# Four mixing layers on one core: long scan pieces beside attention, images normalised ahead, softmax reciprocals by DMA, convolutions summed in place

## The chip, the cores and the metric

The kernel runs on one core of a Trainium2 chip. The metric is the device time of one execution in microseconds: the median of three runs was 4425.56 us (4419.15 to 4431.18). The core has a matrix engine (TensorE, PE in the profile, with its weight loads as PEld), three engines for elementwise work (VectorE or DVE, ScalarE or ACT, GpSimd or POOL), and a queue for transfers (SyncE or SP). Each engine works through its own instructions in the order in which they were issued and waits on semaphores of the others.

## The reference

Four layers follow one another on x of shape (4, 128, 64, 64); each adds its result to x, computed on a group-normalised x. All is float32.

```python
def reference(x, ...):
    ...
    x = x + _L0_conv_ref(_gn(x), ...)   # attention
    x = x + _L1_conv_ref(_gn(x), ...)   # 5x5 convolution
    x = x + _L2_conv_ref(_gn(x), ...)   # selective scan
    x = x + _L3_conv_ref(_gn(x), ...)   # 3x3 convolution
    return x

# layer 0, n = 4096 pixels, c = 128
    scores = jnp.einsum('bic,bjc->bij', q, k) * scale
    attn = jax.nn.softmax(scores, axis=-1)
    out = jnp.einsum('bij,bjc->bic', attn, v)

# layer 2, for each half of the channels (one of them with the pixels reversed)
    delta = jax.nn.softplus(xt @ Wd + bd)
    dA = jnp.exp(delta[..., None] * A)
    dBx = (delta * xt)[..., None] * Bm[:, :, None, :]
    _, h = jax.lax.associative_scan(combine, (dA, dBx), axis=1)   # h = dA * h + dBx
    y = jnp.einsum('bldn,bln->bld', h, Cm) + Dp * xt
```

In layer 3 the branch that depends on an offset returns the same convolution either way.

## The kernel before

Channels lie on the 128 partitions, pixels along the free dimension. A matmul produces 128 x 512 (one PSUM bank of eight); CH = 1024 pixels is a chunk, MM = 512 half of one.

The scan is the long part. `scan_core` walks through 4 images x 256 = 1024 ticks. In tick i ScalarE makes the decay `da` (`decay`, L1261, an exponential), GpSimd the drive `db` (`drive`, L1268), VectorE runs the recurrence over 1024 pixels (`recur`, scan L1278), the product with `cr` is done by VectorE (L1281) or, where `to_pool(i)` says so, by GpSimd (`weigh`, L1299), and TensorE adds the states into `y` (`collect`, L1317, once in four ticks). `da` lies in PSUM. Beside attention and in the preparation it comes as two pieces of 512 from a ring of three banks (pool `s2`, tag `da`, three buffers); beside the convolutions of images 1 to 3 and at the end of the program ("wide") it comes as one piece of 1024 from a pool of two such pieces. A pooled tick writes its states to `hc` at once; any other leaves them in `da` for L1281. The loads of a tick (`load`, L1233 and L1239) go through the SP queue, four ticks ahead (AHEAD).

All else is "work": generators that yield an estimate of TensorE's time. `images()` chains, for each image, `front` (attention, `conv_pairs` for the 5x5 convolution, `scan_prep` for the operands of the scan) and, once the images are in, `back` for the last layer. Between two halves of a tick the main loop draws work for PACE / 2 us (PACE = 2.8; for the last image ENDPACE = 1.5), so PACE fixes how ticks and work are interleaved on every engine; there is no other scheduler. The ticks of an image begin only when `(b, "operands", 0)` is ready. Image 0 is done up to there with no ticks beside it.

Attention takes 256 steps per image, 32 for each of 8 blocks of 512 queries: `scores` (L487) into one of two banks, an exponential on ScalarE (L493) into a ring of eight slots, `values` (L499) two steps later, and each fourth step the column sums `zp` of the softmax on TensorE (`sums`, L521). For image 0 the sums are made on VectorE and GpSimd instead (`side_sums`, L541). At a block's end the sums are turned into columns by tiny matmuls (`turn`, L564), inverted (`invert`, L573 and L575), widened back over the partitions by matmuls (`widen_out`, L479) into bank `z`, and used (`settle`, L587 and L588).

Before an image's attention `attention_start` takes its statistics (L401) and normalises it (L392). This runs in the preparation of the image before.

`conv_pairs` computes pairs of rows: one shared sum of ten products and two sums of 15, one for each row. For images 1 to 3 (`lean`) ScalarE copies the shared sum to SBUF (L982) and TensorE adds it to both others by an identity product (L996). Image 0 goes another way, with more combined rows.

A second copy of the program stands behind a test of the softmax sums; it isn't executed with these inputs.

Of the kernel before, what the change touches and what calls it, by code (L numbers as in the profile page):

```python
# [32 lines left out]
P = 128  # L33
# [12 lines left out]
PRODUCT, HOP, SLOT, PACE, ENDPACE, AHEAD = 0.86, 1.7, 0.7, 2.8, 1.5, 4  # L46
# [6 lines left out]
def conv_preact_kernel(  # L53
# [342 lines left out]

    def attention_start(b, xn):

        st = stats_tile(f"a{b}")
        for i in range(NM):  # L400
            nc.vector.bn_stats(st[:, i, :], xn[:, bass.ts(i, MM)])  # L401
            yield 0.0
        gn = yield from group_norm(st, f"a{b}")
# [6 lines left out]
        def piece(i):  # L410
            cut = bass.ts(i, L // 4)
            normalise(xn[:, cut], xn[:, cut], gn)
# [29 lines left out]
    def attention(b, xs, xn, v, st, safe, loads):  # L442
# [15 lines left out]
        def row_max(blk):  # L458
# [14 lines left out]
            mb[blk] = pools["bg"].tile([P, MM], F32, tag="w", bufs=4, name=f"mb_{b}_{blk}")  # L473
# [69 lines left out]
        def evict_sums(blk):  # L543
            zs = None
            if not fill:
                zs = pools["bg"].tile([P, MM], F32, tag="zs", bufs=1, name=f"zs_{b}_{blk}")
                nc.scalar.copy(zs, zp.pop(blk))
            state[blk] = None, zs

        def evict(blk):  # L550
            raw = pools["bg"].tile([P, MM], F32, tag="raw", bufs=1, name=f"raw_{b}_{blk}")
# [46 lines left out]
        for u in range(N):  # L598
# [11 lines left out]
            if w >= 0:  # L610
# [11 lines left out]
                if d == NJT - 1:  # L622
                    evict_sums(blk - 1)
                    evict(blk - 1)
                    for n, f in ((1, turn), (2, invert), (4, widen_out), (5, settle)):
                        after(u, n, f, blk - 1)
            for f, args in later.pop(u, ()):
                f(*args)
                cost += PRODUCT if f in (turn, widen_out) else 0.0
# [14 lines left out]
        values(N - 4)  # L644
        yield PRODUCT
        while due:
            sums(due.pop(0)[0])
            yield PRODUCT
        for n in range(NRING - 4):
# [185 lines left out]
    def conv_pairs(b, xs, tag, st, st2, lean):  # L835
# [89 lines left out]
        steps, done = [], None  # L925
# [17 lines left out]
        for c in range(L // CH):  # L943
            j = c * CK
            if c < 2:
                piece(2 + c)
            if c < 3:
                differences(c + 1)
            accs = [
                (bank("s", f"pq_{b}_{c}"), ((SUM12, image, 2 * j + 2), (SUM34, image, 2 * j + 4))),  # L950
                (bank("a", f"pe0_{b}_{c}"),
                 ((0, image, 2 * j), (1, diff, j), (3, diff, j + 1))),
                (bank("z", f"pe1_{b}_{c}"),
                 ((0, image, 2 * j + 1), (2, diff, NP + j + 1), (4, diff, NP + j + 2))),
            ]
            if wide:
                total, first, last = (combo(n) for n in range(3))
                accs = [
                    (accs[0][0], (accs[0][1][1], (HSUM, total, j))),
                    (bank("y", f"pm_{b}_{c}"), ((HDIF, diff, j),)),  # L960
                    (accs[1][0], ((0, first, j), (3, diff, j + 1))),
                    (accs[2][0], ((2, last, j), (4, diff, NP + j + 2))),
                ]
            for n, (acc, parts) in enumerate(accs):
                k, total = 0, len(parts) * K5
                for w, view, r in parts:
                    for dx in range(K5):
                        k += 1
                        nc.tensor.matmul(  # L969
                            flat(acc), matrix(w, dx), view(r, dx),  # L970
                            start=k == 1, stop=k == total and (n == 0 or not lean),
                        )
                        if k == 3 and done is not None:
                            done()
                            done = None
                        if k % 3 == 0:
                            yield 3 * PRODUCT
# [697 lines left out]
```

## Time and profile before

| | |
|---|---|
| median of three runs | 4425.56 us (4419.15 to 4431.18) |
| profiled execution, its own time | 4426.94 us |
| its span, first to last instruction | 4425.1 us |
| busy PE / DVE / POOL / ACT | 3896.3 / 3702.6 / 3603.6 / 2377.4 us |
| mean granted clock of TensorE | 0.936 |
| DMA moved | 726.05 MB, 164 GB/s |
| scans and products on VectorE (L1278, L1281) | 1232 pieces of 512 and 408 of 1024 pixels |

Lines are those of the kernel before. A row of a group gives the engine, the operation, output<-inputs, shapes and count; then busy time and mean length of one, then the idle time of the engine just ahead of it and what ended it. In a timeline row the first two numbers are start and length in us. Matmul rows overlap, so a busy PE may hold less work than its share says; distances between starts are safer.

### The profile page before, as it was taken

The numbers are of one execution on the slowest core, as the hardware profiler recorded it, in microseconds if no ns is written. First come the engines' busy times: TensorE is split into PE (matmuls) and PEld (weight loads), VectorE is DVE, ScalarE is ACT, GpSimd is POOL, SyncE is SP. The second block draws the span as 40 slices with busy tenths as digits, with TensorE's granted clock in tenths as the row PEclk, the third lists the DMA queues.
The fourth block names the chain that finished last, engine by engine and source line by source line (L and its number), as shares of the span: only waits on it lengthen the run. The fifth ranks groups of instructions, "written<-read, shape, count | busy, mean of one in ns | idle before, by whom it ended". The sixth has DMA issues, their size and how long they took to land. (4 is left out here: it accounts for less than half of the span.)

```text
span 4425.1 us, 42907 instructions
## 1 busy us (share of the span) xinstructions
PE 3896.3 (88%) x13352; PEld 1486.0 (34%) x13352; DVE 3702.6 (84%) x3471; ACT 2377.4 (54%) x4301; POOL 3603.6 (81%) x1713
## 2 busy tenths in 40 slices
PE   8999997999999979999989889999989657575667
PEld 4444433333333323333333333333333112121212
DVE  4722217999999989999999889999999899999996
ACT  3333217666665376666664576666643754444533
POOL 3433307999999968999989889999999789999995
PEclk9999999999999989999999989999999868787888
DMA  1000016545555565544545564555555666656562
GB/s 64 21 1 1 0 53 231 185 167 176 177 176 182 176 238 198 176 176 168 185 173 181 201 228 168 175 177 175 176 181 177 223 221 206 228 195 232 187 227 84
DMA packets 216302, 726.05 MB, mean 164 GB/s; under 512 B 26240, under 2 KB 27520, under 8 KB 215808
## 3 DMA queue, kind: packets, MB, share of 16 engines
q1 hardware_dynamic: 214144, 722.49, 47.1%
q8 instruction: 107, 1.75, 0.2%
q14 instruction: 131, 1.07, 0.1%
q10 hardware_dynamic: 1920, 0.73, 0.1%
HBM read 653.98 MB, written 69.14 MB: 163 GB/s over the span
## 5 line engine op out<-in xcount | busy, mean ns | idle before, releaser
L1268 POOL TENSOR_TENSOR db<-dx,br 128x1024 f32<-128x1024 f32 x1024 | 2399.5, 2366 | 224.8 <-DMA dx<-dxd 76.7
L1261 ACT ACTIVATE da<-de,a_neg 128x512 f32<-128x512 f32 (+1 forms) x1640 | 1303.1, 797 | 759.6 <-DVE da L1278 305.0
L487 PE MATMUL sc<-r,x 128*128 128x512 f32 x2048 | 1082.2, 611 | 22.5 <-ACT last L1294 9.7
L499 PE MATMUL acc<-exchange,v 128*128 128x512 f32 x2048 | 1048.6, 594 | 2.7 <-ACT raw L552 0.5
L1299 POOL TENSOR_TENSOR hc<-hc,cr 128x1024 f32<-128x1024 f32 x386 | 913.3, 2366 | 22.9 <-ACT last L1294 20.9
L1281 DVE TENSOR_TENSOR hc<-da,cr 128x512 f32<-128x512 f32 (+1 forms) x1003 | 839.5, 837 | 65.7 <-issue 1.3
L1278 DVE TENSOR_TENSOR_SCAN da<-da,last,db 128x512 f32<-128x512 f32 (+1 forms) x480 | 863.1, 1798 | 22.6 <-POOL db L1268 17.7
L493 ACT ACTIVATE exchange<-sc 128x512 f32<-128x512 f32 x1024 | 603.6, 589 | 503.1 <-PE sc L487 494.6
L1317 PE MATMUL y<-hc,sel 128*32 128x512 f32 x4096 | 604.8, 650 | 284.4 <-POOL hc L1299 230.9
L487 PEld LDWEIGHTS sc<-r,x 128*128 128x128 f32 x2048 | 361.8, 190 | 596.5 <-issue 376.7
L499 PEld LDWEIGHTS acc<-exchange,v 128*128 128x128 f32 x2048 | 386.9, 190 | 500.6 <-issue 478.5
L1278 DVE TENSOR_TENSOR_SCAN hc<-da,last,db 128x512 f32<-128x512 f32 (+1 forms) x288 | 490.9, 1705 | 6.4 <-ACT da L1261 3.3
L1278 DVE TENSOR_TENSOR_SCAN da<-da,da,db 128x512 f32<-128x512 f32 x365 | 469.7, 1287 | 6.8 <-ACT da L1261 6.6
L541 POOL TENSOR_TENSOR sidep<-sidep,exchange 128x512 f32<-128x512 f32 x120 | 170.8, 1423 | 273.4 <-ACT exchange L493 271.1
L1317 PEld LDWEIGHTS y<-hc,sel 128*32 128x32 f32 x4096 | 114.4, 113 | 715.5 <-POOL hc L1299 315.2
L1278 DVE TENSOR_TENSOR_SCAN hc<-da,hc,db 128x512 f32<-128x512 f32 x251 | 322.0, 1283 | 32.7 <-ACT da L1261 8.9
L541 DVE TENSOR_TENSOR sided<-sided,exchange 128x512 f32<-128x512 f32 x120 | 95.9, 799 | 221.7 <-ACT exchange L493 220.3
L1278 DVE TENSOR_TENSOR_SCAN da<-da,db 128x512 f32<-128x512 f32 (+1 forms) x158 | 232.4, 1471 | 13.1 <-ACT da L1261 10.1
L703 PE MATMUL pcm<-xpm,cs 128*128 128x512 f32 x432 | 214.5, 646 | 25.2 <-ACT xpm L392 25.2
L969 PE MATMUL pe<-df,exchange 128*128 128x512 f32 x480 | 214.2, 595 | 0.0
L521 PE MATMUL zp<-exchange,ones 128*32 128x512 f32 x1536 | 205.3, 601 | 9.6 <-DVE xs L588 9.5
L1294 ACT COPY last<-da 128x1 f32<-128x1 f32 x474 | 73.8, 156 | 259.7 <-DVE hc L1281 257.2
(239 smaller groups left out, 2838.8 us busy)
## 6 DMA issues: line engine op xcount, KB each, us to landing
br<-bm SPq DMA_DIRECT2D x512, 512.0 KB, 5.2
cr<-cm SPq DMA_DIRECT2D x512, 512.0 KB, 4.0
de<-dd SPq DMA_DIRECT2D x64, 512.0 KB, 4.9
dx<-dxd SPq DMA_DIRECT2D x64, 512.0 KB, 6.2
x<-in_x_dram SPq DMA_DIRECT2D x16, 512.0 KB, 6.0
xs<-in_x_dram SPq DMA_DIRECT2D x16, 512.0 KB, 6.6
xsd<-xs SPq DMA_DIRECT2D x16, 512.0 KB, 6.8
xcd<-xc SPq DMA_DIRECT2D x16, 512.0 KB, 2.9
```

What stands on the lines that cost most here:

```text
L487: nc.tensor.matmul(sc, xn[:, bass.ts(j, P)], rq[blk], start=True, stop=True)
L493: nc.scalar.activation(pt, sc, AF.Exp)
L499: nc.tensor.matmul(acc[blk], v[:, j, :], ring[:, u % NRING, :], start=j == 0, stop=j == NJT - 1)
L541: eng.tensor_tensor(s, s, ring[:, u % NRING, :], ALU.add)
L703: nc.tensor.matmul(acc.rearrange("p (r w) -> p r w", w=W), weights[:, t, :], xp[:, y : y + RPM, dx : dx + W], start=t == 0, stop=t == k * ...
L969: nc.tensor.matmul(flat(acc), matrix(w, dx), view(r, dx), start=k == 1, stop=k == total and (n == 0 or not lean),)
L1261: nc.scalar.activation(da, rep["de", b, c, d, g][:, bass.ts(h, size)], AF.Exp, scale=a_neg[:, at(i)])
L1268: nc.gpsimd.tensor_tensor(dbs[i], rep["dx", b, c, d, g], rows["b", b, c, d, q], ALU.mult)
L1278: nc.vector.tensor_tensor_scan(h, da, db[:, cut], before, ALU.mult, ALU.add)
L1281: nc.vector.tensor_tensor(hc[:, cut], h, rows["c", b, c, d, q][:, cut], ALU.mult)
L1299: nc.gpsimd.tensor_tensor(hcs[i], hcs[i], rows["c", b, c, d, q], ALU.mult)
L1317: nc.tensor.matmul(y[r : r + SG, :], sel, hcs[first + gg][:, bass.ts(h, MM)], start=False, stop=q == NQ - 1, tile_position=(0, r), skip_gr ...
```

## The change

1. `normalise_ahead` takes statistics of images 1 to 3 and normalises them while image 0 is in attention, and writes them to DRAM (`normed`); `start` loads these, and `attention_start` skips both steps for b > 0.
2. In all but the last block of an image, `turn`, `invert` and `widen_out` are replaced: the row sums go to DRAM (`spill`), come back as columns (`gather`), are inverted (`invert_rows`), go out (`put_rows`) and come back broadcast over the partitions (`fetch_rows`); ScalarE copies them to bank `z` at the end of the following block (`stage_rows`), and `settle` follows one step later. For image 0 two added 32-column matmuls make the row sums first.
3. In `conv_pairs` with `lean`, ScalarE copies the shared sum into the bank of the first row's sum; each row's group then accumulates on the bank that holds it already. The identity products are gone.
4. Beside attention and in the preparation, odd ticks get one `da` of 1024 pixels. The three banks are handed out from the left and the right side in turn, so two pieces are held at once. Even ticks keep two pieces of 512; the second is issued at the start of its own tick. Pooled ticks are mostly even ones: 4 of 10 beside attention, as before.
5. PACE is 2.74.

```diff
-PRODUCT, HOP, SLOT, PACE, ENDPACE, AHEAD = 0.86, 1.7, 0.7, 2.8, 1.5, 4
+PRODUCT, HOP, SLOT, PACE, ENDPACE, AHEAD = 0.86, 1.7, 0.7, 2.74, 1.5, 4
...
+    def normalise_ahead(pool):
+
+        for b in range(1, B):
+            t = pool.tile([P, L], F32, tag="ahead", name=f"ahead_{b}")
+            for c in range(NCH):
+                nc.sync.dma_start(t[:, bass.ts(c, CH)], xf[b][:, bass.ts(c, CH)])
+            st = stats_tile(f"a{b}")
+            for i in range(NM):
+                if i % 4 == 0:
+                    yield HOP
+                nc.vector.bn_stats(st[:, i, :], t[:, bass.ts(i, MM)])
+            yield HOP
+            gn = yield from group_norm(st, f"a{b}")
+            for c in range(NCH):
+                cut = bass.ts(c, CH)
+                normalise(t[:, cut], t[:, cut], gn)
+                nc.sync.dma_start(normed[b][:, cut], t[:, cut])
+                yield HOP
...
-        st = stats_tile(f"a{b}")
-        for i in range(NM):
...
+        if b == 0:
+            st = stats_tile(f"a{b}")
...
-            normalise(xn[:, cut], xn[:, cut], gn)
+            if b == 0:
+                normalise(xn[:, cut], xn[:, cut], gn)
...
                 zs = pools["bg"].tile([P, MM], F32, tag="zs", bufs=1, name=f"zs_{b}_{blk}")
                 nc.scalar.copy(zs, zp.pop(blk))
+            elif blk + 1 < NM:
+                zs = pools["bg"].tile([P, MM], F32, tag="zs", bufs=1, name=f"zs_{b}_{blk}")
+                pz = bank("z", f"pz_{b}_{blk}")
+                for g, e in enumerate("dp"):
+                    nc.tensor.matmul(
+                        pz[g * 32 : (g + 1) * 32, :], ones[:, :32], sides.pop((blk, e)),
+                        start=True, stop=True, tile_position=(0, g * 32), skip_group_check=True,
+                    )
+                nc.scalar.copy(zs[:64], pz[:64])
...
+        def spill(blk):
+            raw, zs = state[blk]
+            n = 2 if fill else 4
+            zd = dram.tile([4, MM], F32, tag="zp", name=f"zd_{b}_{blk}")
+            nc.sync.dma_start(zd[:n], zs[0 : n * 32 : 32, :])
...
+        def gather(blk):
+            raw, zd = state[blk]
+            zt = small.tile([P, 4, RUN], F32, tag="zt", name=f"zt_{b}_{blk}")
+            n = zd.shape[0]
+            nc.sync.dma_start(zt[:, :n, :], zd.rearrange("g (p j) -> p g j", j=RUN))
...
+        def invert_rows(blk):
+            raw, zt = state[blk]
+            z = zall[:, b * NJT + blk * TPM : b * NJT + (blk + 1) * TPM]
+            nc.vector.tensor_reduce(z, zt.rearrange("p g j -> p j g"), AX.X, ALU.add)
+            zr = small.tile([P, RUN], F32, tag="zr", name=f"zr_{b}_{blk}")
+            nc.vector.reciprocal(zr, z)
+            state[blk] = raw, zr
...
+        def put_rows(blk):
+            raw, zr = state[blk]
+            zd = dram.tile([P, RUN], F32, tag="zd", name=f"zi_{b}_{blk}")
+            nc.sync.dma_start(zd, zr)
...
+        def fetch_rows(blk):
+            raw, zd = state[blk]
+            rb = pools["bg"].tile([P, MM], F32, tag="w", bufs=4, name=f"rb_{b}_{blk}")
+            row = zd.rearrange("p j -> (p j)").unsqueeze(0)
+            nc.sync.dma_start(rb, row.to_broadcast([P, MM]))
...
+        def stage_rows(blk, tag):
+            raw, rb = state[blk]
+            pb = bank(tag, f"rz_{b}_{blk}")
+            nc.scalar.copy(pb, rb)
+            state[blk] = raw, pb
...
-                    for n, f in ((1, turn), (2, invert), (4, widen_out), (5, settle)):
+                    for n, f in (
+                        (2, spill), (4, gather), (7, invert_rows), (9, put_rows), (11, fetch_rows)
+                    ):
                         after(u, n, f, blk - 1)
+                    if blk > 1:
+                        stage_rows(blk - 2, "z")
+                        after(u, 1, settle, blk - 2)
+                    cost += PRODUCT if fill else 0.0
...
                 f(*args)
-                cost += PRODUCT if f in (turn, widen_out) else 0.0
...
+        stage_rows(blk - 1, "s")
...
+        settle(blk - 1)
...
+        def group(acc, parts, begun=False):
+            nonlocal done
+            k, of_all = 0, len(parts) * K5
+            for w, view, r in parts:
+                for dx in range(K5):
+                    k += 1
+                    nc.tensor.matmul(
+                        flat(acc), matrix(w, dx), view(r, dx),
+                        start=k == 1 and not begun, stop=k == of_all, skip_group_check=lean,
+                    )
+                    if k == 3 and done is not None:
+                        done()
+                        done = None
+                    if k % 3 == 0:
+                        yield 3 * PRODUCT
...
+        def shared_of(c):
+            j = c * CK
+            held[c] = bank("sz"[c % 2], f"pq_{b}_{c}")
+            yield from group(
...
+        def second_of(c):
+            nonlocal done
+            j, acc = c * CK, held.pop(c)
+            yield from group(
+                acc, ((0, image, 2 * j + 1), (2, diff, NP + j + 1), (4, diff, NP + j + 2)), True
+            )
+            done = lambda: add(c, 1, acc)
...
+        def first_of(c):
+            nonlocal done
+            j, acc = c * CK, owns.pop(c)
+            yield from group(
+                acc, ((0, image, 2 * j), (1, diff, j), (3, diff, j + 1)), True
+            )
+            done = lambda: add(c, 0, acc)
...
+        def part(c):
+            owns[c] = bank("a", f"pe0_{b}_{c}")
+            nc.scalar.copy(owns[c], held[c])
...
+        for c in range(NCK + 1 if lean else 0):
+            if c < NCK:
+                advance(c)
+                yield from shared_of(c)
+                done = lambda c=c: part(c)
+            if c > 0:
+                yield from second_of(c - 1)
+            else:
+                yield HOP
+                done()
+                done = None
+            if c < NCK:
+                yield from first_of(c)
...
-                    if lean:
-                        nc.tensor.matmul(acc, ident, qs, start=False, stop=True)
-                        yield PRODUCT
...
+        def part_of_ring(i, h):
+
+            whole = i % 2 == 1
+            if whole and h == 0:
+                return None
+            if turned[0] is not pools["s2"]:
+                turned[:] = pools["s2"], 0
+            side = ("left", "right")[turned[1]]
+            turned[1] = 1 - turned[1]
+            n = CH if whole else MM
+            place = pools["sides"][side]
+            place.close()
+            pool = place.enter_context(
+                tc.tile_pool(name=f"da_{i}_{h}", bufs=1, space=PSUM, side=side)
+            )
+            return pool.tile([P, n], F32, tag="da", name=f"da_{i}_{h}")
...
-                n = i % 5
+                n = i % 10
                 pooled[i] = (
                     i % 3 == 2 if "wide" in pools
-                    else n == 1 if "drives" in ready
-                    else n % 2 == 0 if "operands" in ready else n % 2 == 1
+                    else n % 6 == 2 if "drives" in ready
+                    else n % 2 == 0 or n == 5 if "operands" in ready else n % 2 == 0 and n > 0
...
-            size = CH if "wide" in pools else MM
-            pool = pools.get("wide") or pools["s2"]
-            da = pool.tile([P, size], F32, tag="da", bufs=2 if size == CH else 3, name=f"da_{i}_{h}")
+            if "wide" in pools:
+                da = pools["wide"].tile([P, CH], F32, tag="da", bufs=2, name=f"da_{i}_{h}")
+            else:
+                da = part_of_ring(i, h)
+            if da is None:
+                return
+            size = da.shape[1]
...
+            if i in das and len(das[i]) == 1 and das[i][0].shape[1] < CH:
+                decay(i, 1)
...
-            do(decay, i + 1, 1)
+            if i % 2 == 0:
+                do(decay, i + 1, 1)
...
-            yield from load(xn, b)
+            yield from load(xn, normed[b] if b > 0 else xf[b])
```

## The prediction

> **What bounds the kernel now.** I read the page first: busy shares, then the 40 slices. The first six slices (image 0 before the scan) have a full PE and an idle VectorE; from slice 7 PE, VectorE and GpSimd are all near 9; in the last eight PE falls off.
>
> ```profile
> PE 3896.3 (88%) x13352; PEld 1486.0 (34%) x13352; DVE 3702.6 (84%) x3471; ACT 2377.4 (54%) x4301; POOL 3603.6 (81%) x1713
> PE   8999997999999979999989889999989657575667
> DVE  4722217999999989999999889999999899999996
> POOL 3433307999999968999989889999999789999995
> ```
>
> Then I cut the span by what PE does. The order in which the built program issues its instructions gives the tick at which each stage begins, and the running sum of the 1024 `db` products (L1268) gives the time of a tick. Before: image 0 alone to 684 us; for images 1 to 3 an attention (A: 641, 655, 658 us, 185 to 187 ticks each), a convolution (C: 190, 194, 195 us, 54 or 55 ticks), a preparation (P: about 88 us, 13 to 16 ticks); then the end E (836 us, 252 ticks) and 71 us of tail. The window table for A, C and P of image 2 and for E (columns: window, length, busy PE, PEld, DVE, ACT, POOL, granted clock, DMA):
>
> ```profile
> 1640.00:2295.00 655.00, 633.21 (x2423) 239.09 (x2421) 620.25 (x636) 429.17 (x879) 611.20 (x264) 0.99 0.52 178
> 2295.00:2489.00 194.00, 185.01 (x617) 72.94 (x616) 179.46 (x132) 79.74 (x99) 181.45 (x89) 0.97 0.53 184
> 2489.00:2576.00 87.00, 68.39 (x245) 22.02 (x242) 72.30 (x97) 65.89 (x108) 63.93 (x35) 0.84 0.69 244
> 3518.00:4354.00 836.00, 525.58 (x1632) 155.23 (x1624) 803.60 (x477) 395.25 (x627) 793.01 (x359) 0.78 0.61 211
> ```
>
> In A and C PE is at 97% and 95%, DVE at 95% and 93%; in E DVE and POOL are at 96% and 95% and PE at 63%. Busy matmuls overlap, so I looked at PE's timeline in an A:
>
> ```profile
> 1985.00 0.95 PE L564 MATMUL pz<-zsel,zs 128*128 128x1 f32 x8
> 1985.81 1.10 PE L487 MATMUL sc<-r,x 128*128 128x512 f32 x2
> ...
> 1993.09 1.05 PE L479 MATMUL pzb<-ident,zr 128*128 128x128 f32 x8
> 1993.98 1.02 PE L487 MATMUL sc<-r,x 128*128 128x512 f32 x2
> ...
> 1997.51 1.07 PE L521 MATMUL zp<-exchange,ones 128*32 128x512 f32 x8
> 1998.51 1.13 PE L487 MATMUL sc<-r,x 128*128 128x512 f32 x2
> ```
>
> Products start 0.86 us apart without a hole (the code's PRODUCT), so in A PE is the bound: 516 us of counted work x 1.04 (what the sums cost over their 0.86) + 185 ticks x 0.51 us for `y` + 7 us of values = 638 us against 641 to 658. DVE is just behind. The chain that ended last covers only the last 71 us, which the change leaves alone. So: before tick ~770 time follows PE's work; after it, ticks.
>
> **The change, part by part.**
>
> *Softmax reciprocals.* Removed: the turn (the next `sc` was due at 1984.90 and starts at 1985.81: 0.91 us) and the widening (due 1993.10, starts 1993.98: 0.88 us) in 7 of 8 blocks of each image. In A that is 21 x 1.79 = 38 us on the path. In image 0 the turn has twice the products: 0.91 + 0.86 + 0.88 = 2.65, less two added 32-column products. Their nearest row is `zp`, four in 1.1 us: 0.55; bounds 0.3 and 1.72 (one after the other). 7 x 2.1 = **15 us** off; A **38 us** off. Added on ACT: 28 copies of 0.59 us, hidden (429 of 655 us busy). Added on SP: per block four DMAs (0.55 us of issue each), which this trace has not.
>
> ```profile
> ynd<-ys SPq DMA_DIRECT2D x62, 128.0 KB, 3.1
> br<-bm SPq DMA_DIRECT2D x512, 512.0 KB, 5.2
> ```
>
> The gather must land before `invert_rows`, three steps behind it (a step of A is 655 / 256 = 2.56 us: 7.7 us; in image 0 two products of 0.86: 5.2 us); if not, VectorE stops, with side sums or scans queued behind. [...]by the rows 3.1 + 5.2 = 8.3 behind tick loads. I take the rows: spill and gather are two steps (5.1 us in A) apart, so the spill is down and the gather's 5.2 fits. In image 0 the eight-slot ring of exponentials hides some 8 us. Zero; bounds 0 and 2 us x 28 = 56. SP stands for a third of the span in the wait of `cr` for a GpSimd product (1463 us), and a gather waiting 3 us for its spill delays loads that come only every second tick, 6.8 us apart: nothing.
>
> *Convolutions in place.* 24 identity products go (2 x 4 x 3): 24 x 0.86 = 21 us; ACT copies to PSUM instead of SBUF, same 0.59. The copy has a group of 15 products (12.9 us) to hide in, except once per image (1 us). C has 51 or 52 ticks instead of 54 or 55, so 9 x 0.51 = 4 us of `y` less. **25 us** off, from PE-bound stages.
>
> *Images normalised ahead.* 24 statistics (0.68 us, DVE), 12 normalisations (1.24 us, ACT) and 24 DMAs move from P into image 0's attention, where ACT is 36% and DVE 21% busy from 200 to 500 us; there hidden, without the cover 31 us. An exponential may be 1.24 us late; PE asks for its bank 1.8 us later. P is mostly ACT and waits for it: 5 us per image, **15 us** off (images 1 to 3, loaded in the preparations of 0 to 2).
>
> *Scan in one piece.* 310 ticks become whole, nearly all in A (columns of the groups: count | busy, mean ns).
>
> ```profile
> L1261 ACT ACTIVATE da<-de,a_neg 128x512 f32<-128x512 f32 x1232 | 847.6, 691 | 438.8 <-DVE da L1278 305.0 <-DVE hc L1278 116.8 <-DVE gn_sums L343 8.1
> L1261 ACT ACTIVATE da<-de,a_neg 128x1024 f32<-128x1024 f32 x408 | 455.5, 1117 | 320.8 <-DVE hc L1281 254.4 <-DVE hc L1278 58.6 <-DMA de<-dd 3.5
> L1278 DVE TENSOR_TENSOR_SCAN da<-da,last,db 128x1024 f32<-128x1024 f32 x235 | 550.7, 2344 | 16.2 <-POOL db L1268 12.5 <-ACT da L1261 3.6
> L1278 DVE TENSOR_TENSOR_SCAN da<-da,da,db 128x512 f32<-128x512 f32 x365 | 469.7, 1287 | 6.8 <-ACT da L1261 6.6
> L1281 DVE TENSOR_TENSOR hc<-da,cr 128x512 f32<-128x512 f32 x730 | 505.1, 692 | 42.4 <-issue 0.4 <-PE acc L499 0.4
> L1281 DVE TENSOR_TENSOR hc<-da,cr 128x1024 f32<-128x1024 f32 x273 | 334.4, 1225 | 23.4 <-issue 0.9
> ```
>
> A whole tick saves 2 x 1.28 - 2.34 = 0.22 us of scan and 2 x 0.692 - 1.225 = 0.16 us of product. [...]310 x 0.38 = 118 us by the rows; I take the rows. On PE's path neither is worth anything by itself: it is slack. Ten ticks in A cost DVE 4 split pooled at 2.57, one split unpooled at 3.90, five whole at 3.57: 32 us, 3.20 a tick (before 3.37); with block work 3.27, against PE's 2.74 x 1.04 + 0.51 = 3.36. Before, the two were level.
>
> The price is depth. Three half-pieces ahead become two pieces. The second half waits for the whole piece before it, and the next whole exponential (1.12) can start only when the first half is scanned and must be ready within the second half's 1.28. On ACT 0.7 attention exponentials (0.59) stand between: 0.7 x 0.42 us = 0.3 late at most, in four pairs of five: 0.24 us a pair against a slack of 2 x 0.09 = 0.18. I take zero, since such a stall also lets the queues fill; bounds 0 and 0.7 us a pair.
>
> *PACE 2.74.* Work falls by 2% and so does the work per tick; A keeps its ticks, C loses 3 per image. P of image 3 ends near tick 766 instead of 772, so six ticks more run in E at 836 / 252 = 3.32: **+20 us**.
>
> Sum: -15 - 38 - 25 - 15 + 20 = -73. The profiled execution took 4426.9 (span 4425.1), 1.4 over the median of the runs: 4425.6 - 73 = **4353 us**, 1.6% faster. About 0.3% is what runs from 4419 to 4431 can tell.
>
> **The rivals.** (1) *DVE was the bound in A.* For it: 3.37 a tick plus block work is all of A's tick; against: PE's timeline without holes. Then A falls to PE's own sum, 504 x 1.04 + 185 x 0.51 + 7 = 625 us, 26 per image instead of 13: 40 more, **4313**. (2) *The shallower buffer eats A's gain*: a stall 0.14 us a pair above the slack, over 279 pairs, is 38 us: **4391**. For it: ACT already waits 305 us for DVE's `da`. (3) *The handoff becomes the bound in A, and it ends slower.* The place is VectorE before the whole scan, with ACT stuck behind an exponential that waits for PE during a `y` group (2 us every four ticks). Each 0.1 us a pair over the slack costs 28 us; from 0.26 over it the change loses; at 0.4 over, +112 - 73 = +39: **4465**. Against it: `y` comes every second pair, and VectorE can lag PE by 2 us without loss. (4) *The DMAs hide nothing or the loads collide*, 2 us a block: 56 us, **4409 to 4425**, no change at the worst.
>
> **How the numbers follow.** Forecast 0.60 (alone 4315 to 4390), rival 1 0.13, rival 2 0.13, rival 3 0.10, rival 4 at its worst 0.04. Faster 0.86, within 0.3% 0.04, slower 0.10. The range 4300 to 4410 holds the first, nearly all of the next two, and leaves out rival 3.
>
> **What would show it.** Image 0's first `db` at 650 to 670 us instead of 684; A at 640 us or less with 3.4 us a tick; C near 185; no turn rows but 4 blocks' worth; DVE idle in A up, ended by ACT `da` if rivals 2 or 3 hold; DVE waiting on `zt` if rival 4 does. I am wrong if PE in A shows holes ended by ACT, or if E grows by more than 20 us.

## The result: no change, and where each part went

The changed kernel takes 4426.57 us (median of 12 runs, 4421.49 to 4430.83) where the kernel before took 4425.2 beside it. The ratio is 1.0003, with a 95% interval of 0.9995 to 1.001. The forecast was 4353. The profiled execution has a span of 4427.1 us, against 4425.1.

The page of the changed kernel, in the rows that were read of before:

```profile
PE 3829.3 (86%) x12828; PEld 1416.9 (32%) x12828; DVE 3619.2 (82%) x2851; ACT 2344.1 (53%) x4026; POOL 3609.7 (82%) x1716
PE   8999998999998979999989889999988657475656
DVE  4832217899898978898989889899989899999996
POOL 3433308989898979998989799998999799999995
```

The work did go: TensorE has 67 us less (3896.3 to 3829.3), VectorE 83 us less (3702.6 to 3619.2). The time did not follow, so engines wait where they did not before. To see where, I cut both spans at the first score, the first product of the convolution and the first of the preparation of each image. Times are us from profiled executions; in brackets the scan ticks that fall in the stage, counted as `db` products.

| stage | before | after | difference | forecast |
|---|---|---|---|---|
| start and image 0's attention | 507.4 | 502.1 | -5.3 | -15 |
| convolutions, four | 687.6 | 662.3 | -25.3 | -25 |
| preparations of images 0 to 2 | 290.2 | 274.3 | -15.9 | -15 |
| attentions of images 1 to 3 | 1956.0 (558) | 1990.5 (555) | +34.5 | -38 |
| preparation of image 3, end and tail, to TensorE's last product | 976.6 (267) | 990.4 (273) | +13.8 | +20 |

Four rows are near the forecast or off by 10 us. One has the wrong sign and is off by 72 us: the attentions of images 1 to 3, called A in the prediction. Their tick went from 1956.0 / 558 = 3.51 us to 1990.5 / 555 = 3.59, where 3.4 was forecast. The window table for A of image 2, cut at these points, before and in the changed kernel (same columns as before: window, length, busy PE, PEld, DVE, ACT, POOL, granted clock, DMA):

```profile
1660.88:2313.47 652.59, 630.87 (x2414) 235.83 (x2414) 616.21 (x646) 417.95 (x861) 605.22 (x267) 0.99 0.52 179
1652.72:2317.54 664.82, 628.04 (x2302) 224.78 (x2302) 593.62 (x461) 408.63 (x777) 604.64 (x266) 0.98 0.54 180
```

In A, TensorE is busy for 94% of the time (before 97%) and VectorE for 89% (before 94%). VectorE's 593.62 us over 185 ticks are 3.21 us a tick with the block work in it (forecast: 3.27), yet the tick takes 3.59: neither engine is full. The granted clock is level with before (0.98 and 0.99 in A), so the clock is not the reason. The groups by form (columns: count | busy, mean ns | idle time before, and what ended it):

```profile
L1422 DVE TENSOR_TENSOR_SCAN da<-da,last,db 128x1024 f32<-128x1024 f32 x438 | 1028.1, 2347 | 96.3 <-ACT last L1438 36.1 <-ACT da L1405 34.8 <-POOL db L1412 24.4
L1405 ACT ACTIVATE da<-de,a_neg 128x1024 f32<-128x1024 f32 x718 | 800.4, 1115 | 433.8 <-DVE hc L1425 240.4 <-DVE da L1422 92.2 <-DVE hc L1422 90.1
L1425 DVE TENSOR_TENSOR hc<-da,cr 128x1024 f32<-128x1024 f32 x577 | 706.4, 1224 | 48.7
L1438 ACT COPY last<-da 128x1 f32<-128x1 f32 x474 | 74.8, 158 | 668.1 <-DVE hc L1425 667.4
```

The durations are those that the sum used (2347 ns for a whole scan, 1224 for a whole product). What is new is in the first and the last row. VectorE now waits 36 us for ACT ahead of the whole scan by way of the small copy `last`, which often stands right behind the whole exponential, and 35 by way of the exponential itself. ACT stands 668 us at that copy, which saves the end of a scan, until VectorE's product of the same tick is done, though the copy needs the scan alone. Why it waits for the product too is not shown: the trace shows the wait, and no run took that order away. Before, the same copy had 260 us:

```profile
L1294 ACT COPY last<-da 128x1 f32<-128x1 f32 x474 | 73.8, 156 | 259.7 <-DVE hc L1281 257.2
```

ACT's waits for VectorE are mostly a change of name: before, ACT stood 305 us at the exponential itself for VectorE's scan. What counts is the way back, VectorE waiting for ACT. In A of image 2 (columns of the waits: us in total, times, longest), before:

```profile
DVE da L1278 <- ACT da L1261: 6.6, 7, 2.8
...
DVE hc L1278 <- ACT da L1261: 4.1, 8, 1.1
```

and in the changed kernel:

```profile
ACT last L1438 <- DVE hc L1425: 143.3, 83, 6.4
...
DVE da L1422 <- ACT last L1438: 19.7, 21, 3.8
...
DVE da L1422 <- ACT da L1405: 13.2, 19, 2.2
...
DVE hc L1422 <- ACT da L1405: 4.5, 3, 3.1
```

All of VectorE's waits that ACT ends add up to 11.6 us before and 38.6 us after; TensorE's that ACT ends go from 12.9 to 28.6.

Part of the 38.6 us returns with every tenth tick, and the prediction had nothing for it. Where VectorE takes the product of an even tick, the second scan starts from the last column of the first half, which lies in `da` (in `recur`, `before = h[:, size - 1 : size]`). The next whole exponential then starts only when that second scan has ended:

```profile
1974.73 0.69 DVE L1425 TENSOR_TENSOR hc<-da,cr 128x512 f32<-128x512 f32 x1
1974.73 1.12 ACT L1405 ACTIVATE da<-de,a_neg 128x1024 f32<-128x1024 f32 x1 [1.01 <-DVE da L1422]
1975.79 0.15 ACT L1438 COPY last<-da 128x1 f32<-128x1 f32 x1
1975.95 2.36 DVE L1422 TENSOR_TENSOR_SCAN da<-da,last,db 128x1024 f32<-128x1024 f32 x1 [0.53 <-ACT last L1438]
```

VectorE has a product of 0.69 us left while ACT needs 1.12 and the copy, and it waits 0.53 us. In A of image 2 VectorE waits so after 17 of 19 such ticks, mostly for 0.53 us, 9.6 us in all. In a pooled tick the states lie in `hc`, and the exponential starts beside the second scan, as the first one ends:

```profile
1853.81 1.12 ACT L1405 ACTIVATE da<-de,a_neg 128x1024 f32<-128x1024 f32 x1 [0.24 <-DVE hc L1422]
1853.88 1.28 DVE L1422 TENSOR_TENSOR_SCAN hc<-da,hc,db 128x512 f32<-128x512 f32 x1
```

No run kept that state elsewhere, so what this wait alone is worth was not measured.

The timeline of the changed kernel shows another place, at the end of a block (VectorE, ACT and TensorE only; in brackets the idle time before an instruction and what ended it):

```profile
1982.13 0.67 DVE L664 TENSOR_TENSOR rz<-raw,rz 128x512 f32<-128x512 f32 x1
...
1983.52 0.08 DVE L665 DVE_READ_ACCUMULATOR xs<-rz,bv_c,xs 128x1 f32 x1
1983.64 0.72 ACT L336 ACTIVATE junk<-xs,aw_e 128x512 bf16<-128x512 f32 x1 [2.57 <-DVE xs L665]
...
1984.36 1.10 ACT L1405 ACTIVATE da<-de,a_neg 128x1024 f32<-128x1024 f32 x1
...
1985.40 0.57 ACT L518 ACTIVATE exchange<-sc 128x512 f32<-128x512 f32 x1
1985.56 2.36 DVE L1422 TENSOR_TENSOR_SCAN da<-da,last,db 128x1024 f32<-128x1024 f32 x1 [1.96 <-ACT da L1405]
...
1986.02 2.07 PE L512 MATMUL sc<-r,x 128*128 128x512 f32 x2 [2.92 <-ACT exchange L518]
```

ACT stands 2.57 us at the squares of a settled block (`junk`) because VectorE has not settled it yet. Behind the squares in ACT's queue stand the next whole exponential of the scan and the next one of the attention. So VectorE stops for 1.96 us, and TensorE for 2.92 us. Both engines are late at once.

### The profile page after: what moved, and what is told of

It is laid out like the page before. It is cut to its first block, busy times and chain, and to the rows that moved or that the text cites. A ratio compares the mean times of both kernels' runs of the same rounds, so it can differ in the third digit from the quotient of the medians.

```text
span 4427.1 us, 41260 instructions
## 1 busy us (share of the span) xinstructions
PE 3829.3 (86%) x12828; PEld 1416.9 (32%) x12828; DVE 3619.2 (82%) x2851; ACT 2344.1 (53%) x4026; POOL 3609.7 (82%) x1716
## 5 line engine op out<-in xcount | busy, mean ns | idle before, releaser
L1405 ACT ACTIVATE da<-de,a_neg 128x512 f32<-128x512 f32 (+1 forms) x1330 | 1223.6, 921 | 463.3 <-DVE hc L1425 256.2
L1422 DVE TENSOR_TENSOR_SCAN da<-da,last,db 128x1024 f32<-128x1024 f32 x477 | 1078.1, 2260 | 100.1 <-ACT last L1438 36.1
L512 PE MATMUL sc<-r,x 128*128 128x512 f32 x2048 | 1087.1, 614 | 69.5 <-ACT exchange L518 34.2
L1443 POOL TENSOR_TENSOR hc<-hc,cr 128x1024 f32<-128x1024 f32 x389 | 923.1, 2373 | 6.7 <-ACT last L1438 5.0
L1425 DVE TENSOR_TENSOR hc<-da,cr 128x1024 f32<-128x1024 f32 (+1 forms) x693 | 786.6, 1135 | 55.7
L1438 ACT COPY last<-da 128x1 f32<-128x1 f32 x474 | 74.8, 158 | 668.1 <-DVE hc L1425 667.4
L1422 DVE TENSOR_TENSOR_SCAN da<-da,db 128x1024 f32<-128x1024 f32 (+1 forms) x158 | 341.4, 2161 | 57.3 <-ACT da L1405 28.0
L1039 PE MATMUL pq<-xpe,cs 128*128 128x512 f32 x280 | 137.1, 641 | 40.6 <-ACT xpe L392 40.6
L1176 PE MATMUL pt<-xn,wtap 128*64 128x512 f32 x512 | 127.1, 630 | 33.9 <-ACT xn L392 32.9
```

The lines of the kernel that those rows point to most:

```text
L512: nc.tensor.matmul(sc, xn[:, bass.ts(j, P)], rq[blk], start=True, stop=True)
L1405: nc.scalar.activation(da, rep["de", b, c, d, g][:, cut], AF.Exp, scale=a_neg[:, at(i)])
L1422: nc.vector.tensor_tensor_scan(h, da, db[:, cut], before, ALU.mult, ALU.add)
L1425: nc.vector.tensor_tensor(hc[:, cut], h, rows["c", b, c, d, q][:, cut], ALU.mult)
L1443: nc.gpsimd.tensor_tensor(hcs[i], hcs[i], rows["c", b, c, d, q], ALU.mult)
```

## The experiments

Two theories stood at the start. *Theory D*: the three banks used as a half and a whole piece let any burst on ACT through to VectorE and TensorE, because less is ready ahead of VectorE. *Theory B*: the new reciprocals lengthen the bursts on ACT at block ends and the end of each attention, and would cost the same without the ring. Two more came from the first runs: *T against W* (which engine bounds A without the ring) and *S* (the squares alone make the ring's loss).

"Holes" below are what the starts of TensorE's products in A lie apart beyond their undisturbed distance, where that is over 0.3 us, summed around the ends of blocks (means over images 1 to 3). Before they are 6.3 us an attention, after 16.9. What counts as undisturbed is a choice: with the median distance of each pair of kinds they are 6.4 and 18.4.

**The ring undone (e1).** The changed kernel with the half-pieces, their bank choice and the old choice of pooled ticks back; all else, PACE 2.74 too, stays.

```
-                da = part_of_ring(i, h)
+            da = pool.tile([P, size], F32, tag="da", bufs=2 if size == CH else 3, name=f"da_{i}_{h}")
...
-                n = i % 10
+                n = i % 5
```

> The changed kernel with its ring undone: three half-pieces of da and the old choice of pooled ticks, all else as changed. Theory D (the loss in attention comes from the depth of two pieces, which lets every burst on ScalarE through to VectorE and TensorE): an attention falls from 661 to 665 us to 640 to 650, the whole to about 4365 to 4380. Theory B (the loss comes from the burst at a block's end and the longer end of attention that the reciprocals by DMA bring): attention stays at 660 or more, the whole at 4420 or more.

Measured: 4399.91 us, ratio 0.9941 (0.9924 to 0.9957): the ring costs 27 us, and without it the change is a gain. An attention takes 648.3 us on average where the changed kernel takes 663.5, as theory D had it; the whole stays above D's 4365 to 4380, so the ring is only part of what the forecast missed. (The trace is of this kernel's fastest run, 10.5 us under the median. In e10 below, whose trace lies at its median, an attention takes 649.0: with the ring the three take 43 us more than there, and the other stages 11 less.) The window of A of image 2, and VectorE's waits for ACT in it:

```profile
1638.99:2286.12 647.13, 621.47 (x2302) 222.43 (x2303) 614.11 (x644) 420.30 (x869) 598.90 (x264) 0.99 0.55 184
```

```profile
DVE da L1400 <- ACT da L1383: 3.0, 4, 1.3
DVE hc L1400 <- ACT da L1383: 2.0, 3, 1.5
```

VectorE is busier by 20.5 us (614.11 against 593.62), and that is what the ring saves. But with the ring it waits 31.6 us more for ACT (38.6 against 7.0). In A the ring loses more by waiting than it saves by joining pieces. TensorE's waits that ACT ends are 23.2 us here, so the larger part of their rise, from 12.9 to 28.6, is not the ring's.

**The old reciprocals with everything else of the change (e2).** The lines that make the new ones go as well.

```
-                        (2, spill), (4, gather), (7, invert_rows), (9, put_rows), (11, fetch_rows)
+                    for n, f in ((1, turn), (2, invert), (4, widen_out), (5, settle)):
```

> The changed kernel with the softmax reciprocals made on TensorE again (turn, invert, widen), all else as changed, the ring of two pieces too. Theory D: the holes of TensorE stay, attention is 665 us or more, since 12 us of TensorE work come back; the whole 4430 to 4470. Theory B: the holes at a block's end and at the end of attention fall back to those of before (6 and 11 us), attention about 650 us, the whole about 4385.

Measured: 4449.78 us, ratio 1.0055 (1.0038 to 1.0072). Putting the old way back costs 23 us: the reciprocals by DMA are a gain. Attention takes 676.7 us with 190 ticks, 3.56 a tick, so the ring's long tick is there without the new burst, and theory B does not hold as the main cause.

**The ring alone (e3)**, with its choice of pooled ticks, on the kernel before (PACE 2.8, old reciprocals, images and convolutions as before).

```
+            whole = i % 2 == 1
+            if whole and h == 0:
+                return None
...
-            da = pool.tile([P, size], F32, tag="da", bufs=2 if size == CH else 3, name=f"da_{i}_{h}")
+                da = part_of_ring(i, h)
```

> The kernel before with the ring of two pieces and the new choice of pooled ticks alone (PACE 2.8). Theory D: 15 to 20 us of holes more in each attention, the whole 4460 to 4490. Theory B: VectorE's saving is slack and nothing else changes, 4405 to 4430.

Measured: 4483.24 us, ratio 1.0133 (1.0112 to 1.0155). Alone, the ring costs 58 us. Attention takes 668.1 us against 652.0, with 556 ticks in the three against 558; VectorE's waits for ACT in A of image 2 are 50.2 us. This is theory D's cost on ground where nothing else differs.

**The settling of a block later (e4)**: ACT's copy of the reciprocals and VectorE's settling three steps later, away from the copies of the sums and of the block.

```
-                        stage_rows(blk - 2, "z")
-                        after(u, 1, settle, blk - 2)
+                        after(u, 3, stage_rows, blk - 2, "z")
+                        after(u, 4, settle, blk - 2)
```

> The changed kernel with stage_rows three steps and settle four steps after the end of a block, instead of at once and one step after, so that ScalarE does not make three copies in a row. Theory D: little, within 10 us of 4426. Theory B: the holes of TensorE in steps 2 to 10 of a block fall from about 17 us to 8 us an image, the whole to about 4400.

Measured: 4417.53 us, ratio 0.9982 (0.9973 to 0.999): 9 us better than the changed kernel. TensorE's holes at block ends fall from 16.9 to 10.1 us an attention, but the attention falls only from 663.5 to 659.3 us. Only a part comes from the order at block ends.

**The other choice of pooled ticks (e5, and e6 with the later settling too)**: GpSimd takes the products of the whole ticks instead of the half ones.

```
-                    else n % 2 == 0 or n == 5 if "operands" in ready else n % 2 == 0 and n > 0
+                    else n % 2 == 1 or n == 4 if "operands" in ready else n % 2 == 1 and n < 9
```

> The changed kernel with the pooled ticks moved from the split to the whole ticks (the same share of ticks). A whole pooled tick gives its banks back after the scan (2.34 us) and not after scan and product (3.57), and a split tick that isn't pooled lasts 2 x 1.97 us and not 2 x 1.28, so each exponential has more time; VectorE pays 0.16 us more in 4 ticks of 10. Theory D in this detail (what is late is the exponential behind a piece that is short or held long): attention 640 to 655 us, the whole 4375 to 4405. If only the number of pieces counts: attention 665 us, the whole 4420 to 4440.

> The one before with stage_rows and settle three steps later as well. The later settle gave 8 us with the other choice of pooled ticks; theory D, with the burst bridged by longer pieces: 0 to 5 us faster than the one before. If the two are independent: 8 us faster.

Measured: 4488.69 us, ratio 1.0143 (1.0123 to 1.0163), and 4488.91 us, ratio 1.0139 (1.0119 to 1.0159). Both are misses: the attention grew from 663.5 to 680.5 and 681.0 us. VectorE's waits for ACT in A of image 2 are 60.0 us, 42.4 of them ahead of the scans whose product goes to GpSimd. The expectation took it that a half tick on VectorE leaves each exponential more time. The trace has it the other way round: now most even ticks are of the kind shown at 1974 us, whose second scan starts from a state in the first half's bank, and ACT's exponential waits 127.3 us in 76 waits for a scan into `da` (in the changed kernel 26.8 in 17). In 63 of the 74 pairs with a pooled whole tick the exponential starts within 0.06 us of the end of the second scan, and VectorE waits 0.51 us (median of the 74).

**Two half-pieces (e7).** The kernel before with all its half-pieces, two in flight instead of three. The exponentials are issued later too: the second half when its tick starts, the first half of the next tick behind this tick's scans. No whole pieces, so nothing is saved on VectorE.

```
-            da = pool.tile([P, size], F32, tag="da", bufs=2 if size == CH else 3, name=f"da_{i}_{h}")
+            da = pool.tile([P, size], F32, tag="da", bufs=2, name=f"da_{i}_{h}")
...
+            if i in das and len(das[i]) == 1 and das[i][0].shape[1] < CH:
+                decay(i, 1)
...
+            if not late and "wide" not in pools:
+                do(decay, i + 1, 0)
...
-            do(decay, i + 1, 1)
```

> The kernel before with a ring of two half-pieces instead of three, no whole pieces, nothing else of the change. Theory D: depth alone costs as much as the ring of the change does, and VectorE saves nothing: attention 670 us or more, the whole 4480 to 4520. If the loss comes from the whole pieces (longer waits on ScalarE), not from depth: 4425 to 4445.

Measured: 4653.6 us, ratio 1.051 (1.0488 to 1.0532): one bank less, with the later issue, costs 228 us, far more than the 4480 to 4520 of theory D. The two were not taken apart. The window of A of image 2, and the waits in it:

```profile
1747.89:2457.09 709.20, 649.33 (x2414) 236.07 (x2415) 622.16 (x642) 416.53 (x860) 601.40 (x265) 0.98 0.48 164
```

```profile
ACT da L1261 <- DVE da L1278: 212.6, 110, 2.6
...
DVE hc L1278 <- ACT da L1261: 43.1, 43, 4.7
...
DVE da L1278 <- ACT da L1261: 14.9, 16, 4.0
```

The same kind of wait, larger: VectorE waits 58.9 us for ACT in A, and ACT waits 212.6 us for a scan to release a bank. The ring (e3) has a bank more and whole pieces, and loses 58.

**PACE 2.8 on the changed kernel (e8).**

```
-PRODUCT, HOP, SLOT, PACE, ENDPACE, AHEAD = 0.86, 1.7, 0.7, 2.74, 1.5, 4
+PRODUCT, HOP, SLOT, PACE, ENDPACE, AHEAD = 0.86, 1.7, 0.7, 2.8, 1.5, 4
```

> The changed kernel with PACE 2.8 again. TensorE gets 2% more work per tick, so attention has fewer ticks and the scan's end has about 16 more. If attention is held by a loop of VectorE and ScalarE that goes by ticks (theory D): attention falls by about 2% to 652 us, the end grows by 16 x 3.3 = 53 us, the whole 4420 to 4440. If attention is held by TensorE: it keeps 661 to 665 us, the whole 4445 or more.

Measured: 4453.23 us, ratio 1.0058 (1.0039 to 1.0078). Attention falls only to 658.0 us on average, with 182 ticks of 3.62 us each, and the end grows by 50. The attention lies between the two expectations (652 if ticks hold it, 661 or more if TensorE does), and the whole is in the second one's range. So neither ticks nor products alone set A beside the ring. In the changed kernel, e2, e3 and e8 its tick is 3.56 to 3.62 us, whatever TensorE's work.

**Without the ring: PACE 2.8 (e9), the later settling (e10), the later settling with PACE 2.68 (e11).** These ask what bounds A without the ring. The edits are those shown above, on the kernel with the ring undone.

> The reciprocals, the images and the convolutions alone, with the ring of half-pieces and PACE 2.8 as before. Without the ring at PACE 2.74 an attention takes 648 us where the prediction's sum for PE, with the turns and the widenings gone, is 638. Theory T (without the ring VectorE's ticks are the bound there: 185 ticks of 3.5 us): 2.2% fewer ticks, 4 an attention, take 14 us off each, to 634 us, and the 14 to 16 ticks moved to the end add 3.3 us each, 50 us: about 4400 us, the same as at 2.74. Theory W (PE's work and its holes are the bound): attention stays at 645 to 648 us, and the end's 50 us are all added: 4440 to 4450 us. Against the kernel before (same PACE, same ring) the sum of the prediction's own terms for these three parts is -15 - 38 - 25 - 15 = -93, 4333 us.

> The changed kernel without the ring, and with the copy of the reciprocals three steps and the settling four steps behind a block's end, instead of zero and one. With the ring that step was worth 9 us, taken out of the holes at block ends (16.9 to 10.1 us an attention). Theory D (those holes come of the shallow ring and the burst together): without the ring the holes at block ends are 7 us, and little is left to gain: 4395 to 4402 us. Theory B (the burst alone makes them): again 7 us per attention, 4375 to 4385 us.

> As the run before it, with PACE 2.68: 2.2% more ticks beside the attentions and 15 fewer at the end. Theory T (VectorE's ticks are the bound in attention): each attention grows by 14 us, the convolutions by 4, the end falls by 50: about the same time, 4395 to 4405. Theory W (PE's work is the bound): attention stays, the end falls by 50 us: 4350 to 4360.

Measured: 4410.13 us, ratio 0.9963 (0.995 to 0.9977); 4395.91 us, 0.9931 (0.9917 to 0.9944); 4413.94 us, 0.9975 (0.9965 to 0.9985). The window of A of image 2 with the `db` products in it, that is the ticks (GpSimd alone; window, length, busy and count, granted clock, DMA), at PACE 2.8:

```profile
1632.16:2271.47 639.31, 423.55 (x181) 0.99 0.55 184
```

and at 2.68 with the later settling:

```profile
1651.07:2318.78 667.71, 444.00 (x189) 0.98 0.54 185
```

Means over three attentions are 642.9 us at 181 ticks, 648.3 at 185 (649.0 with the later settling) and 664.6 at 189. From 185 to 189 a tick costs 3.9 us: that fits theory T, with VectorE's ticks as the bound. From 181 to 185 it costs 1.4 us: there theory W, with TensorE as the bound, is nearer. So PACE 2.74 lies near the corner, and neither the 4333 us that the forecast's own terms give at PACE 2.8 nor W's 4350 to 4360 at 2.68 was reached. The later settling gives 4 us here (its interval and that of the kernel without it overlap), within theory D's range and short of theory B's.

**The squares apart**, with the ring (e12) and without it (e13): the squares of a settled block come three steps after the settling.

```
             )
-            st.squares(blk, xs[:, cut], xs[:, 0:1])
+            if not apart:
+                squares(blk)
...
-                        after(u, 1, settle, blk - 2)
+                        after(u, 1, settle, blk - 2, True)
+                        after(u, 4, squares, blk - 2)
```

> The changed kernel with one edit: the squares of a settled block (ACT) are issued three steps after the settling (VectorE) instead of right behind it. In the changed kernel's timeline at 1982 to 1986 us ACT stands 2.57 us at the squares for VectorE's settling, with the next whole exponential and an attention exponential behind it; VectorE then waits 1.96 us and PE 2.92 us. Theory S (most of what the ring costs at block ends is this one wait): PE's holes at block ends go from 16.9 to 8 us an attention or less, an attention from 663 to 652 to 655 us, the whole to 4395 to 4405 us, level with the kernel without the ring. Theory D alone (the loss is the shallow ring's tick, 3.59 us against 3.50, wherever ACT's work stands): the holes move elsewhere, attention stays at 657 to 663 us, the whole at 4415 to 4427 us.

> The same edit without the ring (the half-pieces of the kernel before). There the holes at block ends are 7 us an attention and VectorE's ticks (185 of 3.50 us) are the bound. Both theories: 3 to 5 us an attention at most, 4385 to 4400 us. If theory S holds, this run and the one before it lie within 10 us of each other; if theory D holds alone, 20 us or more apart.

Measured: with the ring 4404.25 us, ratio 0.9956 (0.9942 to 0.9969); without it 4390.86 us, ratio 0.9925 (0.9911 to 0.9938). The two are 13 us apart, between what theory S (10 or less) and theory D alone (20 or more) had; the run with the ring is in S's range for the whole. With the ring, A of image 2 and the waits of VectorE for ACT are:

```profile
1647.60:2304.31 656.71, 624.28 (x2302) 223.46 (x2303) 593.32 (x461) 408.29 (x777) 604.68 (x266) 0.98 0.54 182
```

```profile
DVE da L1428 <- ACT last L1444: 23.3, 22, 3.8
...
DVE da L1428 <- ACT da L1411: 9.7, 16, 1.4
```

The attention fell from 663.5 to 656.5 us on average, and the holes at block ends from 16.9 to 9.8. But VectorE still waits 35.6 us for ACT, at other places, and without the ring the attention is 649.7. The edit brings 22 us with the ring. Without it the median falls by 9 (4399.91 to 4390.86), but the intervals overlap and the attention is no shorter, where 3 to 5 us were expected. The gap between the two kernels closes from 26.7 to 13.4 us, so roughly half of the ring's loss is this one wait for the settling. The other half is spread over the ticks: of the 35.6 us, 10.4 come behind the even ticks whose product is VectorE's, as shown at 1974 us. The kernel without the ring and with the squares apart has the lowest median of all, 0.75% below the kernel before.

One row sums up the runs. VectorE's waits that ACT ends, in A of image 2: without the ring 5.1 to 11.6 us in six kernels (before, e1, e9, e10, e11, e13); with it 34.2 to 50.2 in six (after, e2, e3, e4, e8, e12); with the whole ticks pooled 60.0 (e5); with two half-pieces 58.9 (e7).

## Why the prediction was wrong, point by point

*Scan in one piece: this step failed.* The prediction bounded the stall at 0 and 0.7 us a pair, and said "I take zero, since such a stall also lets the queues fill". In A of image 2 VectorE waits 27.0 us more for ACT than before (38.6 - 11.6), over 92 pairs of ticks 0.29 us a pair, and the three attentions are 45 us longer than without the ring (e1). The reason given for zero is what the runs contradict. It took it that TensorE goes on while VectorE stalls. But ACT serves both from one queue in order: while it stands at something that VectorE holds, the attention's exponentials stand behind it, as at 1983 us above (ACT 2.57 us, TensorE 2.92). The estimate of 0.24 us late against 0.18 of slack also averaged over all pairs what comes in single waits of up to 3.8 us, which no slack of 0.09 us a tick absorbs. And it counted four pairs in five: the fifth, where VectorE takes the product of the half tick, was put at nothing without a reason and has 0.53 us nearly every time. Undoing the ring brings back 27 of the 73 us that are missing; the reciprocals in A, next, are the largest part of the rest. The saving on VectorE itself was right: whole pieces save 2 x 1.283 - 2.347 = 0.22 us of scan and 2 x 0.691 - 1.224 = 0.16 of product, as the rows of before gave it.

*Reciprocals, 38 us in A: present in TensorE's work, not in the time.* TensorE has 112 instructions fewer in A of image 2 (2414 to 2302). With PACE left at 2.8 and no ring, three attentions gave back 27 of the 38 us (1956.0 to 1928.7), but the shorter work carried fewer ticks and the end took 22 more, 65 us: all parts without the ring together gained only 16 us over the whole kernel (e9). With PACE 2.74 and no ring it was 11 us in A (1945.0), where VectorE and TensorE are busy for 95% and 96% of A (e1) and neither has much room. The gain needed a shorter tick as well. That was the ring's part, and the ring made the tick longer.

*The DMAs hide: right.* The sum that waits for the gathered row, `zall<-zt`, finds VectorE idle before it once in 28 times, for 0.5 us, in image 0. Rival 4, with the author's estimate of 2 us a block, is out.

*Reciprocals in image 0, 15 us: mis-sized.* TensorE's block takes 57.55 us instead of 58.74, so 1.19 us a block are saved where 2.1 were forecast, 7 us over the six blocks that can be told apart. The last block with the attention's end takes 71.9 us instead of 71.6, so there the saving is lost again, and the first score comes 1.35 us later: the row of the table is left with 5.3. Why the end and the start are longer was not looked into. The two 32-column products were taken at 0.55 us, by the nearest row:

```profile
145.72 0.62 PE L577 MATMUL pz<-sided,ones 128*32 128x512 f32 x1
145.72 0.62 PE L577 MATMUL pz<-sidep,ones 128*32 128x512 f32 x1
146.17 0.59 PE L577 MATMUL pz<-sided,ones 128*32 128x512 f32 x1
146.18 0.59 PE L577 MATMUL pz<-sidep,ones 128*32 128x512 f32 x1
146.70 1.13 PE L512 MATMUL sc<-r,x 128*128 128x512 f32 x2
147.96 1.13 PE L524 MATMUL acc<-exchange,v 128*128 128x512 f32 x2
148.92 1.02 PE L512 MATMUL sc<-r,x 128*128 128x512 f32 x2
```

The pair takes 0.98 us (145.72 to 146.70), a little more than one full product (0.86). The product behind it takes 1.26 us to the next start instead of 0.86, and the one after it 0.96. Beyond the 1.72 us of two products elsewhere, that is 1.48 us in all. The four products of `zp` were 1.1 us as one group, and a quarter each was the wrong reading: here the two start together (145.72 and 145.72), and they cost nearly what the four cost, 0.98 us to the next start against 1.00 (1997.51 to 1998.51 in the timeline of before). The later successor comes on top; no run shows the reason for it.

*Convolutions 25 us, images 15 us, PACE 20 us: about right, but not taken one by one.* Their rows of the table have 25.3 and 15.9 us, and for PACE six more ticks at the end (267 to 273) and 13.8 us. No run has the convolutions or the images alone, and the ring and PACE act on the preparations as well. Setting PACE back beside the rest of the change (e8) lost 27 us, so 2.74 was a gain there. The images cost nothing in image 0's attention: with the old reciprocals and the images ahead it takes 479.3 us, as before (479.2).

*The rivals.* None gave 4427. Rivals 2 and 3 named the mechanism and what would show it (VectorE idle in A, ended by ACT; TensorE with holes ended by ACT), and both signs are there. For the size some luck is in it. A came out 72.5 us above the forecast, 0.26 us over each of 279 pairs, the point from which rival 3 has the change lose. But only 45 of these, 0.16 us a pair, came with the ring (e1), which is rival 2's size; the other 27 are the reciprocals' missing gain, which no rival had. The two had 0.23 of the chance. What was held against rival 3, "VectorE can lag PE by 2 us without loss", was the author's estimate, without a row of its own.

## What to carry to other kernels

When two streams share one in-order queue, a buffer between that queue and a third engine is not only that engine's slack: where it is too short, the queue stands still and the other stream can stall with it (at 1983 us here ACT stood 2.57 us, VectorE 1.96 and TensorE 2.92). Judge an edit that trades depth for fewer instructions by the idle time that comes back from the producer (VectorE's waits that ACT ends), not by the busy time that it saves, and look in the producer's queue for instructions that wait for the consumer, such as the squares here: moving them was worth 22 us with the ring and no more than the noise without. Ask also which later instruction still reads a buffer, such as a scan that takes its start from the piece before it (mostly 0.53 us of waiting here), before counting that buffer as free. When work that carries a background loop is cut, count where the loop's ticks go, since they have to run elsewhere.

## What the runs showed of the hardware that was not expected

- The full product behind two products of 32 columns side by side takes 1.26 us to the next start, against 0.86 elsewhere in image 0's attention (the changed kernel at 146.70 us).
- One half-piece less in flight between ACT and VectorE (two instead of three), with the exponentials issued later, cost 228 us, 5%, with the durations the same: ACT's exponential of a half-piece takes 0.69 us and VectorE's scan of it 1.28, in e7 as before.
- A scan of 512 pixels that takes its start value from the piece before it held ACT's next exponential in the ring back until it ended: behind such ticks VectorE waited, mostly for 0.53 us, 17 times of 19 in one attention (image 2 of the changed kernel).
